# Two cross-attention layers on one core: 120-row chunks in the first layer, transposes issued earlier and singly, a normalisation shared among three engines

## Chip, core, metric

One Trainium2 chip, one core of it. The metric is the device time of the whole kernel in microseconds (us): the median of three runs, and beside it one profiled execution, whose trace gives every other number here. Data are fp32 throughout.

## What is computed

Eight batches. `x` is (8, 100, 1024), the context (8, 1444, 512). Layer 0 is softmax attention over the context with an output projection and a residual; layer 1 is attention whose softmax runs over the 100 queries (axis 1), with a residual and a layer norm.

```python
# layer 0
Q = query @ Wq + bq; K = key @ Wk + bk; V = key @ Wv + bv
weights = softmax(Q @ K.T * 1024**-0.5, axis=-1)
x = query + (weights @ V) @ Wo + bo
# layer 1
q = emb @ Wq + bq; k = latent @ Wk + bk; v = latent @ Wv + bv
w = softmax(q @ k.T / sqrt(1024), axis=1)     # over the queries
x = w @ v + emb
out = (x - mean) * rsqrt(var + 1e-6) * gamma + beta
```

## The kernel before

The kernel multiplies weights together first (Wq with Wk, Wv with Wo), so that scores come straight from `x` and the context, and it forms weights times context (`A`, 512 wide) before it multiplies by the value weights. The large products of weights and the projections use seven half-size products instead of eight (`weight_products`, `queries`, `seven_products`, all through `half_product`, L125). `xT` holds x transposed (1024 features in 8 blocks of 128 partitions, 800 query columns) and takes both residuals.

**Order of work.** TensorE's instructions run in the order in which the program states them (`manual_schedule(engines={PE})`, L65). The other engines' instructions are put in order by the framework's planner, which works with its own costs and may take a later instruction first when an earlier one is not ready; each engine then runs its list strictly in that order. SyncE (SP) issues the context's loads. Loads go into `stream`, ten units that rotate. `bank` gives one of six PSUM banks in turn, `bank2` one of two others.

**First layer.** `scores0` (L493) makes one batch's scores, 44 matmuls, each two issues of TensorE: queries g0T stationary (100 columns), 131 or 132 context columns moving. It yields after each matmul, so that its steps can be put between others. At its last step it emits the softmax: ScalarE evicts (L519), VectorE takes maxima (L520), ScalarE does the exponential (L524) and scales (L527) in `prob`, 100 queries by 1444 positions. The weights must then be transposed, with positions on partitions. `transposed` (L533) has VectorE do this in 32x32 blocks (L542, 16 instructions of up to 12 blocks). For batches 0 and 7, `first_transposed` (L552) has TensorE transpose the first four chunks (L557, `PT = 4`), and ScalarE copies them (L558).

`weighted_rows` (L470) then forms A over 12 chunks of positions: 48 matmuls (L476), context stationary (128 columns), 100 columns of weights moving, one step each. In the first layer a chunk has 128 positions, and the last one 36 (`held_full`), loaded by `load_full_rows` (L430). In the second layer chunks have 120 positions, the last one 124 (`held`), loaded by `load_rows` (L443), which reads 128 rows a chunk at a step of 120 rows.

The main loop of layer 0 first makes the scores of batches 0 and 1 and calls `first_transposed(batches[0])`. Then for each batch b it puts one step of A of b and one step of scores of b+2 alternately (two of the latter at b = 5); the batches 6 and 7 have A alone. `first_transposed(batches[7])` is called at the end of batch 6. `project0` follows.

**Second layer.** `scores1` (L604) has positions on partitions from the start. `attend1` (L670) and, for batches 6 and 7, `weighted_rows` form A. `attended` (L691) transposes it; in batches 6 and 7 ScalarE copies A into A1T directly (L487). `project1_halves` adds the projection of batches 0 to 4 into xT at the end of batch 5; `project1` (L717) that of 5 and 6 at the end of batch 6, eight blocks e of four matmuls (L723), each added by VectorE (L727); it calls `between` after the fourth. `project_last` (L767) does batch 7 (`ol`, L774).

`finish` (L761) makes a batch's output. `untransposed` (L731): eight transposes of TensorE (L738) in two banks, from xT back to 100 rows, and after each four VectorE adds the bias (L740). `statistics`: L745. `normalise` (L747): mean and variance (L750), plus EPS (L752) on VectorE; GpSimd takes the power -1/2 (L753); VectorE forms (z - mean) * gamma (L754), then z * rstd + beta (L758); GpSimd issues the DMA of the output (L759). In batch 7 that last part goes in two halves, issued by SP and ScalarE. `finished` says at which step of which batch `finish` is called whole: batches 0, 1, 2, 3 at steps 0, 12, 26, 40 of batch 6; 4 in the middle of `project1`; 5 and 6 at steps 0 and 16 of batch 7.

## Time and profile before

| | us |
|---|---|
| median of three runs | 662.25 (662.13 to 662.52) |
| the profiled execution | 659.84 |
| its span, first to last instruction | 658.1 |
| first layer's loop, from the first score to project0 | 193.0 to 357.3 |
| last stage, from batch 6 of layer 1 on | 600.8 to 658.1 |
| granted TensorE clock, mean | 0.996 |

Rows of the profile name an engine (PE is TensorE's matmul, PEld its weight load, DVE VectorE, ACT ScalarE, POOL GpSimd, SP SyncE, and a q after it the engine's own queue), the line of the kernel, the operation, the tiles as output<-inputs, the shape, and how many (x). A group's row then has busy time and mean ns of one, and after a second bar the idle time of the engine before it and who ended it. A timeline's row starts with its start and its length in us and merges instructions of the same kind that follow each other. The ends of matmuls are modelled, so the distance between starts says more of TensorE's pace than the lengths.

### The profile page before, as it was taken

To read this page: it belongs to the slowest core of one execution; us is meant where nothing else is said; L and a number is where in the kernel's file an instruction comes from. 1 tells how busy PE (TensorE), PEld (TensorE's weight loads), DVE (VectorE), ACT (ScalarE), POOL (GpSimd) and SP (SyncE) were. 2 spreads that over 40 slices of the span, in tenths; PEclk is the share of its full clock that TensorE was granted. 3 is DMA by queue.
4 is the path that set the end of the run, shared out by engine and by line. 5 is a ranking of instruction groups with operands and counts; after the bars stand their busy time and mean duration, and the time that the engine had idled before them with its cause. 6 is when DMAs were issued, how large, how long until landed. Compare 5 with 4: busy or idle time off the path is not lost.

```text
span 658.1 us, 10293 instructions
## 1 busy us (share of the span) xinstructions
PE 645.4 (98%) x4272; PEld 545.2 (83%) x4272; DVE 404.5 (61%) x771; ACT 120.1 (18%) x313; POOL 27.3 (4%) x37
## 2 busy tenths in 40 slices
PE   9999999999999999999999999999999999999994
PEld 8885445568899999999998555589999999989992
DVE  5979638996054765566742874268344433567994
ACT  1110100321104223321310000214222323210000
POOL 5000000000000000000000000000000000001331
PEclk9999999999999999999999999999999999999998
DMA  9937046000098788888998003038899999810221
GB/s 300 378 123 263 0 129 248 1 0 1 12 355 293 255 290 301 302 300 293 346 330 275 0 0 128 0 105 269 282 313 298 313 293 298 305 58 1 86 66 50
DMA packets 59402, 126.06 MB, mean 192 GB/s; under 512 B 3800, under 2 KB 22744, under 8 KB 59356
## 3 DMA queue, kind: packets, MB, share of 16 engines
q1 hardware_dynamic: 56910, 118.38, 52.4%
q0 software_dynamic: 2048, 6.56, 3.2%
q8 instruction: 33, 0.54, 0.3%
q10 hardware_dynamic: 398, 0.47, 0.2%
q14 instruction: 13, 0.11, 0.0%
HBM read 122.12 MB, written 3.28 MB: 191 GB/s over the span
## 4 chain that ended last, share of the span: by engine, by line
PE 93%; DVE 4%; DMA 1%; issue 1%; POOL 0%; SPq 0%; ACT 0%; POOLq 0%; DVEq 0%
PE A L476 14%; PE s L506 12%; PE s L622 12%; PE A L678 10%; PE qk_x L125 6%; PE g_x L125 5%; PE qk_y L125 4%; PE o_x L125 4%; PE g_y L125 3%; PE vo_x L125 3%; PE o_y L125 3%; PE qk_w L125 2%; PE qk_z L125 2%; PE vo_y L125 2%; PE g_z L125 2%; PE g_w L125 2%
## 5 line engine op out<-in xcount | busy, mean ns | idle before, releaser
L476 PE MATMUL A<-w,c 128*128 128x100 f32 (+1 forms) x960 | 143.9, 269 | 1.2 <-ACT w L558 1.2
L476 PEld LDWEIGHTS A<-w,c 128*128 128x128 f32 (+1 forms) x960 | 127.9, 190 | 3.3 <-ACT w L558 1.6
L622 PE MATMUL s<-g1T,cT 128*120 128x100 f32 (+1 forms) x768 | 123.2, 261 | 0.0
L506 PE MATMUL s<-cT,g0T 128*100 128x131 f32 (+1 forms) x704 | 119.3, 276 | 0.0
L678 PE MATMUL A<-c,w 120*100 120x128 f32 (+1 forms) x576 | 110.7, 273 | 0.0
L622 PEld LDWEIGHTS s<-g1T,cT 128*120 128x120 f32 (+1 forms) x768 | 105.1, 185 | 0.6 <-issue 0.3
L506 PEld LDWEIGHTS s<-cT,g0T 128*100 128x100 f32 x704 | 86.8, 167 | 0.0
L542 DVE STREAM_TRANSPOSE w<-prob 32x352 f32<-32x352 f32 (+3 forms) x128 | 66.5, 519 | 15.3 <-ACT prob L527 12.5
L678 PEld LDWEIGHTS A<-c,w 120*100 120x100 f32 (+1 forms) x576 | 74.0, 168 | 0.0
L642 ACT ACTIVATE w<-w,negmax 120x100 f32<-120x100 f32 (+1 forms) x96 | 35.1, 366 | 75.3 <-DVE negmax L640 75.3
L632 DVE SCALAR_TENSOR_TENSOR w<-s,c 120x400 f32<-120x400 f32 (+1 forms) x24 | 13.8, 573 | 41.6 <-PE s L622 41.6
L519 ACT ACTIVATE prob<-s,c 100x394 f32<-100x394 f32 (+2 forms) x32 | 17.8, 562 | 98.7 <-PE s L506 98.4
L520 DVE TENSOR_REDUCE maxima<-prob 100x1 f32<-100x394 f32 (+2 forms) x32 | 16.4, 528 | 24.3 <-ACT prob L519 24.0
L125 PE MATMUL qk_x<-qk 128*128 128x256 f32 x128 | 28.7, 381 | 0.2 <-DMA qk<-in_L_xattn_WkT 0.2
L125 PEld LDWEIGHTS qk_x<-qk 128*128 128x128 f32 x128 | 23.9, 190 | 4.5 <-issue 0.6
L645 DVE RECIPROCAL rtotal<-total 120x4 f32<-120x4 f32 (+1 forms) x24 | 4.2, 176 | 28.2 <-ACT w L642 28.2
L753 POOL TENSOR_TENSOR rstd<-rstd,mhalf 100x1 f32<-100x1 f32 x8 | 11.8, 1477 | 230.6 <-DVE rstd L752 230.6
L564 DVE TENSOR_TENSOR xT<-xT,o_x 128x400 f32<-128x400 f32 (+1 forms) x24 | 13.7, 603 | 8.3 <-PE o_x L125 7.9
L267 DVE SCALAR_TENSOR_TENSOR qk_L_xattn_bk<-qk,L_xattn_bk,qk_L_xattn_bk 128x1024 f32<-128x1024 f32 x14 | 17.9, 1281 | 0.0
L642 ACT ACTIVATION_READ_ACCUMULATOR w<-w,negmax 120x1 f32 (+1 forms) x96 | 17.9, 186 | 0.0
L659 DVE TENSOR_REDUCE part<-w 120x100 f32<-120x1100 f32 x8 | 17.2, 2147 | 0.0
L332 DVE SCALAR_TENSOR_TENSOR kb<-xT,wqbk,kb 128x400 f32<-128x400 f32 x28 | 16.9, 629 | 0.2
(202 smaller groups left out, 852.8 us busy)
## 6 DMA issues: line engine op xcount, KB each, us to landing
c<-in_ctx SPq DMA_DIRECT2D x48, 768.0 KB, 6.1
cT<-in_ctxT SPq DMA_DIRECT2D x32, 728.0 KB, 6.2
cT<-in_ctxT SPq DMA_DIRECT2D x32, 722.0 KB, 6.4
c<-in_ctx SPq DMA_DIRECT2D x16, 512.0 KB, 8.0
vo<-in_L_xattn_Wo SPq DMA_DIRECT2D x8, 512.0 KB, 5.7
qk<-in_L_xattn_WqT SPq DMA_DIRECT2D x8, 512.0 KB
qk<-in_L_xattn_WqT SPq DMA_DIRECT2D x15, 256.0 KB, 5.4
qk<-in_L_xattn_WkT SPq DMA_DIRECT2D x15, 256.0 KB, 5.8
```

Source lines behind the costliest of these rows:

```text
L125: nc.tensor.matmul(banks[n // per][:, n % per * width : (n % per + 1) * width], lhs[i][:, n * P : (n + 1) * P], rhs[i], start=(fresh and i ...
L267: nc.vector.scalar_tensor_tensor(acc, src, cols[v][:, h : h + 1], acc, ALU.mult, ALU.add)
L332: nc.vector.scalar_tensor_tensor(acc, src, wqbk[:, k : k + 1], acc, ALU.mult, ALU.add)
L476: nc.tensor.matmul(ps[:, k * T : (k + 1) * T], c[m // CQ][:r, m % CQ, k * P : (k + 1) * P], w[:r, m, :], start=(m == 0 and k == 0), stop=( ...
L506: nc.tensor.matmul(banks[n // PM][:T, CUTS[n] - o : CUTS[n + 1] - o], q0[:, k, t0 : t0 + T], cT[k][:, CUTS[n] : CUTS[n + 1]], start=(k == ...
L519: nc.scalar.activation(p[:, o:e], ps[:T, : e - o], AF.Identity, bias=c0[:, b : b + 1], scale=SCALE)
L520: nc.vector.tensor_reduce(parts[:, n : n + 1], p[:, o:e], AX.X, ALU.max)
L542: nc.vector.transpose(blocks(w, r, m0 * T + q * QD, T, n), blocks(p, q, m0 * P + r * QD, P, n),)
L622: nc.tensor.matmul(ps[:r, (m - m0) * T : (m - m0 + 1) * T], cT[m // CQ][:, k, o : o + r], q1[:, k, t0 : t0 + T], start=(k == 0), stop=(k = ...
L642: nc.scalar.activation(w[:r, m, :], w[:r, m, :], AF.Exp, bias=negmax[:r, m : m + 1], accum_out=total[:r, m : m + 1])
L659: nc.vector.tensor_reduce(part[:MR], w[:MR, :last, :].rearrange("p c t -> p t c"), AX.X, ALU.add)
L678: nc.tensor.matmul(ps[:T, part], w[:r, m, :], c[m // CQ][:r, m % CQ, part], start=(m == 0 and k == 0), stop=(m == MC - 1), skip_group_chec ...
```

## The change

It has three parts. The first layer uses `load_rows` and chunks of 120 rows too, `held` everywhere; `load_full_rows` and `held_full` go, and `prob` is 1448 instead of 1472 columns wide. `first_transposed` of batch 0 is called after 40 of the 44 score matmuls of batch 1, and that of batch 7 after 44 of the 48 steps of batch 6, so that four steps follow it. `untransposed` becomes a generator that yields after each transpose; the loop of layer 1 keeps a list of finishing batches and advances each by one transpose after each step of A. Batches 0, 1, 2 start at steps 0, 14, 28 of batch 6, batch 3 is finished whole ahead of `project1`, 4 in its middle as before, 5 and 6 start at steps 6 and 22 of batch 7. z of batches 3 to 5 lies in other buffers (tag gT). In `normalise`, for all batches but the last, ScalarE multiplies z by rstd and GpSimd adds beta, where VectorE did both in L758.

```diff
-SC = -(-S // P)
-SW = (SC - 1) * P + 2 * QD
+SW = (MC - 1) * MR + P
...
-    def load_full_rows(b):
...
-    def held_full(c):
...
-    def weighted_rows(w, c, dst, name, held):
+    def weighted_rows(w, c, dst, name):
...
             for r in range(P // QD):
-                n = SC - m0 - (r * QD >= S % P)
                 nc.vector.transpose(
-                    blocks(w, r, m0 * T + q * QD, T, n),
-                    blocks(p, q, m0 * P + r * QD, P, n),
+                    blocks(w, r, m0 * T + q * QD, T, MC - m0),
+                    blocks(p, q, m0 * MR + r * QD, MR, MC - m0),
                 )
...
         for m in range(PT):
-            nc.tensor.transpose(ps[:, m * T : (m + 1) * T], p[:, m * P : (m + 1) * P], ident[:T, :T])
-        nc.scalar.copy(s["rows"][:, : PT * T], ps[:, : PT * T])
+            nc.tensor.transpose(ps[:MR, m * T : (m + 1) * T], p[:, m * MR : (m + 1) * MR], ident[:T, :T])
+        nc.scalar.copy(s["rows"][:MR, : PT * T], ps[:MR, : PT * T])
...
     def untransposed(s):
         b = s["b"]
-        z = s["z"] = row(f"z_{b}")[:T]
+        if b in range(3, 6):
+            z = work.tile([P, LC, GT], F32, tag="gT", name=f"z_{b}", bufs=3).rearrange("p c t -> p (c t)")[:T, :E]
+        else:
+            z = row(f"z_{b}")[:T]
+        s["z"] = z
         for j in range(2):
             ps = bank(f"z_{b}_{j}")
             for e in range(4):
                 nc.tensor.transpose(ps[:T, e * P : (e + 1) * P], xT[:, 4 * j + e, b * T : (b + 1) * T], ident)
+                if (j, e) != (1, 3):
+                    yield
             half = slice(j * 512, (j + 1) * 512)
             nc.vector.scalar_tensor_tensor(z[:, half], bv1[:T, half], s["r"], ps[:T, :], ALU.mult, ALU.add)
+        yield
...
         nc.vector.scalar_tensor_tensor(z, z, mv[:, 0:1], gamma[:T], ALU.subtract, ALU.mult)
-        parts = 2 if b == B - 1 else 1
-        for j in range(parts):
-            w = slice(j * E // parts, (j + 1) * E // parts)
+        if b < B - 1:
+            nc.scalar.activation(z, z, AF.Copy, scale=rstd)
+            nc.gpsimd.tensor_tensor(z, z, beta[:T], ALU.add)
+            nc.gpsimd.dma_start(out=out[b], in_=z)
+            return
+        for j in range(2):
+            w = slice(j * E // 2, (j + 1) * E // 2)
             nc.vector.scalar_tensor_tensor(z[:, w], z[:, w], rstd, beta[:T, w], ALU.mult, ALU.add)
-            (nc.scalar if j else nc.gpsimd if parts == 1 else nc.sync).dma_start(out=out[b][:, w], in_=z[:, w])
+            (nc.scalar if j else nc.sync).dma_start(out=out[b][:, w], in_=z[:, w])

     def finish(s):
-        untransposed(s)
+        yield from untransposed(s)
...
-    for b in range(2):
-        run(scores0(batches[b], *loaded(load_features(b))))
-    first_transposed(batches[0])
+    run(scores0(batches[0], *loaded(load_features(0))))
+    s0 = scores0(batches[1], *loaded(load_features(1)))
+    for n in range(LC * NP):
+        next(s0)
+        if n == LC * NP - PT - 1:
+            first_transposed(batches[0])
     for b in range(B):
...
-        c, *cT = loaded(load_full_rows(b), *([load_features(b + 2)] if nxt else []))
+        c, *cT = loaded(load_rows(b), *([load_features(b + 2)] if nxt else []))
...
-        if b == B - 2:
-            first_transposed(batches[B - 1])
+            if (b, n) == (B - 2, MC * LC - PT - 1):
+                first_transposed(batches[B - 1])
...
-    finished = {(B - 2, n): (d,) for d, n in enumerate((0, 12, 26, 40))}
-    finished.update({(B - 1, 0): (G1,), (B - 1, 16): (G1 + 1,)})
+    finished = {(B - 2, 0): 0, (B - 2, 14): 1, (B - 2, 28): 2, (B - 1, 6): G1, (B - 1, 22): G1 + 1}
+    finishing = []
...
-            for d in finished.get((b, n), ()):
-                finish(batches[d])
+            if (b, n) in finished:
+                finishing.append(finish(batches[finished[b, n]]))
+            finishing = [f for f in finishing if next(f, finishing) is not finishing]
...
         if b == B - 2:
-            project1(G1, 2, A1[G1][0], lambda: finish(batches[G1 - 1]))
+            run(finish(batches[G1 - 2]))
+            project1(G1, 2, A1[G1][0], lambda: run(finish(batches[G1 - 1])))
```

## Prediction

> **What bounds the kernel now.** I read the page first, then the waits of TensorE, then the timeline of TensorE around each edit, then ScalarE, VectorE and GpSimd in the last 60 us.

> ```profile
> PE 645.4 (98%) x4272; PEld 545.2 (83%) x4272; DVE 404.5 (61%) x771; ACT 120.1 (18%) x313; POOL 27.3 (4%) x37
> ```

> TensorE bounds it: 645.4 of 658.1 us. Some 8 us lie at the start, and 9 us at the end, where the last batch is normalised. Between them its waits that the change can reach are three kinds, 2.9 us in all, shown by the next fence (groups of instructions, columns: busy, mean ns, idle before and who ended it; then two answers of the waits):

> ```profile
> L476 PE MATMUL A<-w,c 128*128 128x100 f32 x704 | 112.8, 266 | 1.2 <-ACT w L558 1.2
> ...
> L476 PE MATMUL A<-w,c 36*128 36x100 f32 x64 | 9.1, 282 | 0.0
> ...
> L738 PE MATMUL z<-ident,xT 128*100 128x128 f32 x64 | 8.5, 273 | 1.2 <-DVE xT L727 1.2
> ...
> PE z L738 <- DVE xT L727: 1.2, 1, 1.2
> PE o L723 <- ACT A1T L487: 0.5, 1, 0.5
> ```

> But a busy TensorE need not be at its pace, so I compare starts. Timeline of TensorE, first layer, the end of batch 0 (start, length, row):

> ```profile
> 232.11 0.39 PE L506 MATMUL s<-cT,g0T 128*100 128x131 f32 x2
> 232.33 0.36 PE L476 MATMUL A<-w,c 128*128 128x100 f32 x2
> 232.53 0.39 PE L506 MATMUL s<-cT,g0T 128*100 128x132 f32 x2
> 232.85 1.53 PE L476 MATMUL A<-w,c 36*128 36x100 f32 x10
> 234.22 0.39 PE L506 MATMUL s<-cT,g0T 128*100 128x131 f32 x2
> ...
> 605.71 3.27 PE L476 MATMUL A<-w,c 120*128 120x100 f32 x28
> 608.81 1.04 PE L738 MATMUL z<-ident,xT 128*100 128x128 f32 x8
> 609.69 3.27 PE L476 MATMUL A<-w,c 120*128 120x100 f32 x28
> ```

> The x10 row holds the eight issues of the 36-row chunk and the next batch's first two. It takes 234.22 - 232.85 = 1.37 us; in the second layer, with 120 rows, 28 such issues take 3.10, 0.111 each, so ten take 1.11. Excess 0.26. Its entry is late too: 0.32 after the s row, where the one before has 0.22. So a 36-row chunk costs **0.36 us a batch** and shows as busy time. Transposes take (609.69 - 608.81)/8 = 0.110 each.

> [...] 36 rows among 128 rows cost 0.36 us for going in and out, while 120 among 128 (second layer) cost nothing visible. [...] here 190 ns with 128 rows, 192 with 120, so 120 rows are no slower. [...]

> **The change, part by part.**

> *Chunks of 120 rows.* There are 12 chunks of either kind, so the same 48 matmuls a batch. Gone is the switch: 8 batches by 0.36 = **-2.9 us**, all on TensorE. Added: loads of 11x128+124 = 1532 rows for 1444, 0.18 MB a batch (+6%), three DMAs on SP for the last quarter instead of two (SP spends 0.4 us on one and is idle for microseconds between them). VectorE's block transposes are all 12 blocks long (568 ns) where half had 11 (538): 64 by 0.03 = 2 us of VectorE spread over 150 us, with 11.8 of 20 us busy in a stage. Both are hidden: a row quarter is issued some 20 us before its use (10 units, 2 used per quarter of a batch) and lands in 6 to 8 us; the second layer moves as many bytes per batch now, at 283 to 307 GB/s and a DMA share of 0.85 to 0.93, and TensorE has no wait there. If the cover were gone: 6.1 MB at 300 GB/s is 20.3 us against a new batch of 19.55, 0.8 us for each of six batches.

> *TensorE's own transposes ahead.* Rows:

> ```profile
> 212.85 0.51 PE L557 MATMUL pT<-ident,prob 100*128 100x100 f32 x4
> 214.00 0.47 PE L476 MATMUL A<-w,c 128*128 128x100 f32 x2 [0.64 <-ACT w L558]
> ...
> 345.06 0.56 PE L557 MATMUL pT<-ident,prob 100*128 100x100 f32 x4
> 346.21 11.13 PE L476 MATMUL A<-w,c 128*128 128x100 f32 x96 [0.58 <-ACT w L558]
> ```

> Four transposes take 0.35, so A could start 0.80 earlier in the first place and 0.74 in the second (0.06 there belongs to the switch above); a first pair after a wait takes 0.30 where later ones take 0.20, 0.10 more each. Sum **-1.7 us**. Now 8 issues follow the transposes: 8 by 0.113 = 0.91 us (scores) or 8 by 0.112 = 0.90 (A), against 0.80 and 0.74 needed. The spare is only 0.1. In the first place ScalarE also evicts batch 1's scores then, at 211.31 to 213.56 without a pause (L519); with the transposes put in after step 40, its third eviction becomes ready later than the copy, so the copy fits between. If it were queued last, 0.9 comes back. The inputs were ready: batch 0's softmax ended at 207.8.

> *Batches one transpose at a time.* Three gains on TensorE:
> (a) finish(3) now stands between the last sums and project1: eight transposes, 0.87 us, fill the wait for the copy of A1T. Row starts 615.21 and 615.95 are 0.74 apart, where 0.11 is due: **-0.6**.
> (b) finish(5) goes from step 0 to step 6 of batch 7. Its eighth transpose now starts at 630.12, seven having started from 627.96 on: 627.96 + 7 x 0.11 = 628.73 was due, **-1.4**. It waits for VectorE's last L727 at 629.71, late because VectorE is full (14.93 of 15 us in 601 to 616, 12.63 of 13 in 616 to 629). The eighth transpose moves 13 steps, 3.5 us, back, and L758 leaves VectorE.
> (c) Mixing. After a group of eight transposes the first two A issues start at 634.70 and 634.79, 0.09 apart, where in a run of A it is 0.112: I read it as room left by the transposes' shorter weight loads. A transpose that stands alone gives that 0.022 each time, a group of eight once. 5 batches by 7 by 0.022 = **-0.8** (between 0 and -0.8; I take -0.8, as the first layer's s and A pairs show it: 0.20 for an A pair among s, 0.224 alone).

> What moves off VectorE: seven L758 of 1.28 us, 9 us, no gain by itself. ScalarE gets seven scalings of 100x1024: L527 takes 1499 ns for 1444, L407 956 for 800, so 1.15 us (estimate, from the slope). GpSimd gets seven adds: [...]

> Gross: 2.9 + 1.7 + 0.6 + 1.4 + 0.8 = **7.4 us**.

> *What is late next.* ScalarE is in order. For each batch the scaling waits for GpSimd's rstd, and behind it stands the copy A1T (L487), for which TensorE waits. In batch 7: from the last transpose of batch 6 to A1T's readiness are 18 steps of 0.224 plus 0.36 = 4.4 us. The scaling's readiness: before, from L740 (636.33) to the end of the pow (640.32) 4.0 us, 0.3 ahead of it; 0.6 less if the first half's statistics no longer come last[...]: 3.7 to 5.1. A tie, so whichever is queued first. If the scaling is (likelier: it comes first in the program), A1T is 0.5 to 1.9 late, less 0.2 that it has to spare (copy ended 642.34, ol started at 642.58). I take **+0.7**. At the end of batch 6 there are 12 steps, 3.0 us, so the copy is ready clearly first; I take 0 and keep 1.6 for the rival.

> Net 7.4 - 0.7 = 6.7. The profiled execution, 659.84 around a span of 658.1, would be 653.1. The median of the runs, 662.25, stands 2.4 above that; the same 6.7 off gives **655.5**.

> **Rivals.**
> 1. *ScalarE's copies become the wait* (chance 0.22). A1T stands behind a scaling in batch 6 (1.6 us) and in batch 7 (1.1), and VectorE[...] leaves no more of (b) than 1.0. For: the tie above, VectorE's full stretch. Against: VectorE gives 9 us away, and ScalarE's queue has already put a ready copy (L558, 213.45) ahead of an exponential that the program has earlier. 655.5 + 1.6 + 0.4 + 0.4 = 657.9.
> 2. *The change does not do what it says in the first layer* (0.07): the copies of part two stay behind other work, or transfers come late. Without part two's 1.7 and with one batch's 0.8: 658.0. All six batches together would be 4.8 us late, less than the 12 us that a quarter has to spare between landing and use.
> 3. *GpSimd becomes the end* (slower; 0.05). Its queue runs from the first pow, about 600, to the last batch's pow, due at 651.08 - 7.4 = 643.7. In 43.6 us stand seven pows and seven DMA issues, 14.4 us, so an add may take 4.2 us. Beyond that each adds seven times its excess to the tail: at 5.2 us the gain is gone, at 6 us the time is 655 + 7 x 1.8 = 667.5. For: no such add was ever timed in the trace. [...]

> **Numbers.** Forecast 655.5, own range 654.2 to 656.9: 0.60. More gain than that (tie goes the other way, a little more from VectorE): 0.06. The rest are the rivals. The range 653.9 to 658.6 leaves out 0.05 below, rival 3, and a little of rival 1. About 0.2%, 1.3 us, is what a measurement of this kernel can tell from no change: faster 0.92, same 0.03, slower 0.05.

> **What would show it.** Right: no L476 row of 36 rows, batches of the first layer 0.36 us apart less; no idle before L476 by L558; no gap at L723 by L487 and none at L738 by L727; transposes in single rows of x1 between pairs of A[...]. Wrong: a wait of ol (L774) or o (L723) on L487 over 1 us, with a scaling just before it on ScalarE; GpSimd busy without a pause up to the tail; a DMA as releaser in the first layer.

## The result and the profile after

| | before | changed |
|---|---|---|
| median, us | 662.19 (661.92 to 662.52, 4 runs) | 653.48 (652.97 to 654.13, 4 runs) |
| profiled execution | 659.84 | 653.41 |
| its span | 658.1 | 651.6 |

The ratio is 0.9869, interval 0.9852 to 0.9886: 8.7 us less. 655.5 was forecast, with 653.9 as the lower end. The two profiled executions differ by only 6.4 us, and that is the riddle of this case: the changed kernel's profiled execution agrees with its median, the one of before stood 2.4 us under its own.

First the stages of the two profiled executions. Each ends where the first matmul of the next starts; the sums are the spans. "Middle" runs from project0 to batch 6 of the second layer, "end" from the first matmul of `project_last`.

| us | to first score | first layer | middle | batch 6 | project1 | batch 7 | end |
|---|---|---|---|---|---|---|---|
| before | 193.00 | 164.27 | 243.49 | 15.19 | 11.81 | 14.82 | 15.49 |
| changed | 193.87 | 160.21 | 243.40 | 14.13 | 11.70 | 13.08 | 15.24 |
| difference | +0.87 | -4.06 | -0.09 | -1.06 | -0.11 | -1.74 | -0.25 |

Without the first column, which the change doesn't touch, 7.3 us are gone; the prediction's sum was 7.4 before its deduction of 0.7.

Page of the changed kernel, engines and the first group (A is L458 now, L476 before):

```profile
PE 641.9 (99%) x4272; PEld 544.1 (84%) x4272; DVE 401.1 (62%) x764; ACT 128.2 (20%) x320; POOL 39.3 (6%) x44
...
L458 PE MATMUL A<-w,c 120*128 120x100 f32 x960 | 145.0, 267 | 0.0
```

No idle time is left before A. Timeline of TensorE, the first transposes of its own (L538) and the end of batch 0:

```profile
212.82 0.51 PE L538 MATMUL pT<-ident,prob 100*120 100x100 f32 x4
213.17 1.07 PE L488 MATMUL s<-cT,g0T 128*100 128x132 f32 x8
214.07 0.36 PE L458 MATMUL A<-w,c 120*128 120x100 f32 x2
...
232.57 0.39 PE L488 MATMUL s<-cT,g0T 128*100 128x132 f32 x2
232.80 1.25 PE L458 MATMUL A<-w,c 124*128 124x100 f32 x10
233.89 0.39 PE L488 MATMUL s<-cT,g0T 128*100 128x131 f32 x2
```

A starts 0.90 us after the first of the eight score issues that now follow the transposes, which is just their own time, 8 by 0.113; no bracket of a wait stands behind its row. The x10 row takes 233.89 - 232.80 = 1.09 us (1.37 before), and it starts 0.23 after the s row (0.32 before): 0.37 us a batch.

The last stage on TensorE (transposes of the outputs are L727, project1 is L704):

```profile
606.94 0.28 PE L727 MATMUL z<-ident,xT 128*100 128x128 f32 x1
607.05 0.36 PE L458 MATMUL A<-w,c 120*128 120x100 f32 x2
607.25 0.27 PE L727 MATMUL z<-ident,xT 128*100 128x128 f32 x1
...
610.64 0.27 PE L647 MATMUL wsum_ps<-ident,wsum 124*100 124x124 f32 x1
610.74 1.04 PE L727 MATMUL z<-ident,xT 128*100 128x128 f32 x8
611.62 5.58 PE L704 MATMUL o<-A1T,wv 128*128 128x200 f32 x32
```

A single transpose and its pair of A take 0.311 us; alone the pair takes 0.223 (issues 0.112 apart in the run of 36 at 631.43), so a transpose costs 0.088 instead of 0.110. project1 starts without a wait, right after the eight transposes of batch 3.

And ScalarE, where I had feared for the copy A1T (L469) behind the scaling (L748):

```profile
631.11 1.15 ACT L748 ACTIVATE z<-z,rstd 100x1024 f32<-100x1024 f32 x1 [5.58 <-POOL rstd L745]
635.68 0.49 ACT L469 COPY A1T<-A 128x400 f32<-128x400 f32 x1 [3.42 <-PE A L458]
636.23 1.15 ACT L748 ACTIVATE z<-z,rstd 100x1024 f32<-100x1024 f32 x1
```

The copy of batch 7 went first, the scaling of batch 6 after it. The loss of 0.7 did not come.

### The profile page after: what moved, and what is told of

Same layout as the page of the kernel before. It is cut to its first block, busy times and chain, and to the rows that moved or that the text cites. A ratio compares the mean times of both kernels' runs of the same rounds, so it can differ in the third digit from the quotient of the medians.

```text
span 651.6 us, 10319 instructions
## 1 busy us (share of the span) xinstructions
PE 641.9 (99%) x4272; PEld 544.1 (84%) x4272; DVE 401.1 (62%) x764; ACT 128.2 (20%) x320; POOL 39.3 (6%) x44
## 4 chain that ended last, share of the span: by engine, by line
PE 58%; issue 35%; POOL 4%; DMA 1%; SPq 0%; POOLq 0%; ACT 0%; DVE 0%; DVEq 0%
PE A L458 12%; PE s L488 12%; PE qk_x L124 6%; PE qk_y L124 4%; PE vo_x L124 3%; PE o_x L124 3%; POOL z L749 3%; PE g_x L124 3%; PE qk_w L124 2%; PE qk_z L124 2%; PE vo_y L124 2%; PE g_y L124 2%; PE o_y L124 1%; PE vo_w L124 1%; PE vo_z L124 1%
## 5 line engine op out<-in xcount | busy, mean ns | idle before, releaser
L458 PE MATMUL A<-w,c 120*128 120x100 f32 x960 | 145.0, 267 | 0.0
L458 PEld LDWEIGHTS A<-w,c 120*128 120x128 f32 x960 | 130.1, 191 | 0.0
L523 DVE STREAM_TRANSPOSE w<-prob 32x384 f32<-32x384 f32 (+1 forms) x128 | 68.6, 536 | 15.3 <-ACT prob L509 12.5
L745 POOL TENSOR_TENSOR rstd<-rstd,mhalf 100x1 f32<-100x1 f32 x8 | 7.5, 934 | 216.5 <-DVE rstd L744 216.4
```

The costliest lines, as they stand in the source:

```text
L458: nc.tensor.matmul(ps[:, k * T : (k + 1) * T], c[m // CQ][:r, m % CQ, k * P : (k + 1) * P], w[:r, m, :], start=(m == 0 and k == 0), stop=( ...
L523: nc.vector.transpose(blocks(w, r, m0 * T + q * QD, T, MC - m0), blocks(p, q, m0 * MR + r * QD, MR, MC - m0),)
```

## The experiments

There are two questions. Do the parts add up as TensorE's stages say, and where do the 2.4 us in the runs of before come from? Theory 1 has it that the stages add up and that the runs of before had something that the profiled execution had not. The rival is a gain that sits outside the stages. Each experiment ran beside the kernel before on the same chip, and the ratios are to these runs.

### The parts alone

`before_again` is the kernel before.

> The kernel before, unchanged. Theory 1 (the profiled execution of before was itself a quick one): its executions spread, and a time near 662.2 us goes with a span near 660.4; the extra is found in a stage that the change doesn't touch, or in the first transfers. Theory 2 (the execution of before was typical, and its runs carry some 2.4 us outside the span): the span is 658 again, with 662 around it.

`rows120`: only the first layer's `load_rows`, `held`, blocks at a step of `MR`.

> Only the first layer's 120-row chunks. Theory 1 (TensorE's stages add up): -2.4 us, which is what the first layer's stage lost in the changed kernel (4.05) without the 1.7 of the transposes ahead; the prediction's own term was -2.9. Theory 2 (part of the gain that the profiles don't show sits in the first layer's loads): -4 to -5 us.

`ahead`: only the two calls of `first_transposed` moved.

> Only TensorE's own transposes earlier, with 128-row chunks. Both theories: -1.7 us, the two idle times before L476 by L558 gone. If the copy fell behind ScalarE's evictions in the first place: -0.8.

`finish`: only `untransposed`, `normalise`, `finish` and their steps.

> Only the finishing: single transposes, new steps, ScalarE and GpSimd in the normalisation. Theory 1: -2.9 (1.06 in batch 6, 0.11 in project1, 1.74 in batch 7), perhaps 0.2 more at the end. Theory 2 (part of the unseen gain sits in the end): -5 us.

| us | median | beside before's 660.63, ratio | first layer | batch 6 | project1 | batch 7 | end |
|---|---|---|---|---|---|---|---|
| before_again | 662.03 | 1.0006 (0.9994 to 1.0018) | 164.26 | 15.19 | 11.81 | 14.81 | 15.48 |
| rows120 | 658.22 | 0.9952 (0.9939 to 0.9965) | 161.94 | 15.20 | 11.81 | 14.82 | 15.47 |
| ahead | 658.96 | 0.9969 (0.9957 to 0.9981) | 162.57 | 15.20 | 11.81 | 14.82 | 15.48 |
| finish | 657.51 | 0.9944 (0.9931 to 0.9957) | 165.89 | 14.13 | 11.71 | 13.08 | 15.20 |

The medians fall by 2.4, 1.7 and 3.1 us, 7.2 in all, and the stages by 2.33, 1.70 and 3.2: theory 1 for the parts. (The intervals of the ratios are about 0.8 us to either side, so the stages are the sharper evidence.) Two things were not expected. The executions of before spread over 2.6 us, from 659.96 to 662.53. And the one profiled of `finish`, which doesn't touch the first layer, has 1.6 us more in it, which the row of the table shows and which is left out of the 3.2. In before_again's own profiled execution (662.12) the extra 2 us are in the first transfers: TensorE stood 1.9 us before its second weights.

### What the row count costs

In the kernel before, the last chunk gets 72 or 64 rows instead of 36 (the diff is shortened):

```diff
# last72, last64: KL = 72 or 64
-        return min(P, S - c * P)
+        return P if c < SC - 1 else KL
...
+                nc.sync.dma_start(out=t[S % P : KL, n, :], in_=src[: KL - S % P, :])
```

> The kernel before with a last chunk of 72 rows instead of 36: rows 36 to 71 carry other rows of the context with weights of zero, so that the result is the same. Theory 1 [...]: -2.9 us, all in the first layer's stage, 164.3 to 161.4, a little under the 161.9 of 120-row chunks. Rival (the unequal chunk, or its separate DMA, costs the time): no change.

> The same with 64 rows. Theory 1: [...] no gain: stage 164.3. If the cost came from any number of rows under some other bound, between 161.4 and 164.3.

Timeline of TensorE at the end of batch 0, last64, then last72:

```profile
233.82 0.39 PE L508 MATMUL s<-cT,g0T 128*100 128x132 f32 x2
234.14 1.53 PE L478 MATMUL A<-w,c 64*128 64x100 f32 x10
235.50 0.39 PE L508 MATMUL s<-cT,g0T 128*100 128x131 f32 x2
```

```profile
233.76 0.39 PE L508 MATMUL s<-cT,g0T 128*100 128x132 f32 x2
233.99 1.26 PE L478 MATMUL A<-w,c 72*128 72x100 f32 x10
235.08 0.39 PE L508 MATMUL s<-cT,g0T 128*100 128x131 f32 x2
```

64 rows: 0.32 to enter and 1.36 for ten, as 36 had. 72 rows: 0.23 and 1.09, as 124 have. The first layer took 164.25 with 64 and 161.51 with 72; the ratios to before are 0.9996 (0.9988 to 1.0005) and 0.995 (0.9935 to 0.9964). So the whole cost hangs on the number of rows: it is there at 36 and at 64 and gone at 72, 2.76 us for eight chunks. The rival falls: the unequal chunk and its extra DMAs are still there in last72. Why 36 and 64 rows have it and 72 have not is not shown. The traces show only the delay, and put 0.35 us on going in and out: in the trace of before the issues of the chunk of 36 rows start 0.11 apart, the first and second at either change of rows 0.20 to 0.21 and 0.19 after the one ahead.

120-row chunks took 161.94, 0.43 more than last72. `both72` is the changed kernel with that last chunk, `after_third` the changed kernel beside it.

> The changed kernel's other two parts with the first layer in 128-row chunks whose last one has 72 rows (36 of them with weights of zero), in place of 120-row chunks. Theory 1 ([...] 120-row chunks give back 0.4 us of pace): the first layer's stage 159.8 in place of 160.2, the rest as in the changed kernel, so 0.4 us less than it. Rival (no difference that can be seen): 160.2 and the same time.

> The changed kernel once more, on the chip of both72, to compare with it. Theory 1: 653.0 to 653.6, in one group, with a clock of 1.00 through the first layer, whatever the runs of before do; its first layer's stage 160.2.

First layer 159.79 against 160.21, every other stage within 0.06. The medians are 652.78 (652.57 to 652.85) and 653.41 (653.02 to 654.15): the four runs of each don't overlap. both72 is the best of all kernels here, 0.9877 (0.9861 to 0.9894) of before on its chip. One round of two score issues and two of A takes 0.4258 us with 120-row chunks and 0.4240 with 128-row ones, on average over some 185 rounds of either trace; the stage has some 240 of them, which makes the 0.43. Why is open.

### Who removed the wait of batch 5

`no_share` is the changed kernel with L748 and L749 put back on VectorE:

```diff
-            nc.scalar.activation(z, z, AF.Copy, scale=rstd)
-            nc.gpsimd.tensor_tensor(z, z, beta[:T], ALU.add)
+            nc.vector.scalar_tensor_tensor(z, z, rstd, beta[:T], ALU.mult, ALU.add)
```

> The changed kernel with rstd and beta on VectorE in one instruction as before. Theory 1 (moving the step off VectorE gains nothing by itself once finish(5) is later): TensorE's stages as in the changed kernel, batch 6 14.13, project1 11.70, batch 7 13.08; its tail the same within 0.3. Rival (VectorE's relief is what removes the wait of the eighth transpose): batch 7 0.5 to 1.5 us longer.

`share_only` is the kernel before with the reverse edit, finishes whole and at the old steps.

> The kernel before with ScalarE and GpSimd in the normalisation, whole finishes at the old steps. Theory 1: batch 6 and project1 as before (15.2 and 11.8); in batch 7 some of the 1.4 us of waiting on L727 goes, since VectorE ends its adds earlier: 13.4 to 14.2 in place of 14.8. Rival ([...] the adds are no earlier): 14.8 or more.

`steps_0_16` is the changed kernel with batches 5 and 6 from steps 0 and 16.

> The changed kernel with batches 5 and 6 finished from steps 0 and 16 of batch 7, as before, but singly. Theory 1: the eighth transpose of batch 5 is at 625.5, after VectorE's last add at 624.5, so no wait; the scaling of batch 6 now comes ahead of the copy A1T on ScalarE and delays it by 0 to 0.5: batch 7 13.1 to 13.5. Rival (the later steps are what removed the wait): 14 or more.

| us | ratio to before on its chip | batch 6 | project1 | batch 7 | end |
|---|---|---|---|---|---|
| changed (after_third) | 0.9888 (0.9873 to 0.9902) | 14.13 | 11.71 | 13.08 | 15.17 |
| no_share | 0.9903 (0.9887 to 0.992) | 14.13 | 12.02 | 13.89 | 15.50 |
| steps_0_16 | 0.9879 (0.9858 to 0.9901) | 14.13 | 11.71 | 13.16 | 15.27 |
| before | 1 | 15.19 | 11.81 | 14.82 | 15.49 |
| share_only | 0.9981 (0.9973 to 0.999) | 15.20 | 11.81 | 13.38 | 15.21 |

All waits of TensorE from the first score on, no_share and then share_only:

```profile
PE z L727 <- DVE xT L708: 0.6, 1, 0.6
```

```profile
PE A L476 <- ACT w L558: 1.2, 2, 0.6
PE o L723 <- ACT A1T L487: 0.5, 1, 0.5
```

In batch 7 of no_share half of the wait is back, six steps later notwithstanding (0.6 where the kernel before has 1.2), and its project1 is 0.31 longer too: weight loads there wait 0.3 for L708. share_only has no wait for VectorE's L727 at all. Its batch 7 is 1.44 shorter than before, the whole of the 1.4, and steps_0_16 loses 0.08 without the later steps. So the rival holds: VectorE's relief is enough to take the wait away, the later steps (with the transposes one at a time) take half of it by themselves, and with the relief they are spare. The 0.08 of steps_0_16 is the tie that I had feared, the other way round: there the scaling of batch 6 runs first, the copy behind it, and the first weights of `ol` wait 0.2 for the copy.

```profile
635.00 1.15 ACT L748 ACTIVATE z<-z,rstd 100x1024 f32<-100x1024 f32 x1 [3.98 <-POOL rstd L745]
636.06 0.47 ACT L469 COPY A1T<-A 128x400 f32<-128x400 f32 x1
```

### The 2.4 us: a window at half clock

In the profiled execution of `finish` the granted clock of TensorE (the share of full speed that it was given) was 0.5 for 3.4 us in the first layer, right behind the second wait for L558. The kernel before has these waits, the changed one has not. These runs were made to see whether the waits do it:

`gap_longer`, the kernel before with a loop of four around the copy.

> The kernel before with the copy L558 done four times, 1.2 us more at both places where TensorE waits for it. Theory 1 (such a wait can make the clock that is granted to TensorE fall to half for 3.4 us, as one execution showed right after this wait): +2.4 us from the waits, and where the clock falls 1.7 us more each time; the windows show a clock under 1 after 214 or 346. Rival (that fall of the clock had nothing to do with the wait): +2.4 and a clock of 1.00 there.

`filled`, the kernel before with work in place of the idle time:

```diff
+        fill = bank(f"fill_{b}")
+        for _ in range(3):
+            nc.tensor.matmul(fill[:, :P], ones, ones, start=True, stop=True)
         nc.scalar.copy(s["rows"][:, : PT * T], ps[:, : PT * T])
```

> The kernel before, with three matmuls of ones (never read) put on TensorE after each of the two groups of its own transposes, so that it works through most of the wait for L558; nothing becomes earlier. Theory 1 (in about half of the executions of before the wait costs a window of 3.4 us at half clock): times near 660.2 throughout, none of the group near 662, clock 1.00 in the stage. Rival (the two groups of times of before come from elsewhere, for example from the first transfers): two groups as before.

`no_ahead`, the changed kernel with the calls back in place:

> The changed kernel with the calls of first_transposed put back to where they were. Theory 1: both waits are back, 1.7 us, and with them the window at half clock in some executions: times near 654.8 and near 656.6. Rival: +1.7 throughout, one group.

Two more executions of before with a trace, and the changed kernel again:

> The kernel before, another execution with its trace. Theory 1: if its time is near 660, the clock is 1.00 in the whole first layer; if it is near 662, the clock is at half for 3.4 us after 214 or 346, or the first transfers were 2 us late (as in the execution of before_again).

> The kernel before, one more execution with its trace. Theory 1: a time near 660 goes with a clock of 1.00 through the first layer, a time near 662 with half clock for 3.4 us after 214 or 346, or with first transfers that are 2 us late.

> The changed kernel, unchanged. Theory 1 (the terms add up, and the runs of before shown with the result were drawn high): 653.4 again, against a median of before near 660.8: -7.3 us, ratio 0.989. Rival (the gain is 8.7): ratio 0.987 again.

The two executions took 661.85 and 661.95 us. TensorE around the second wait in before_look1, ahead of it the last chunk of batch 6:

```profile
344.78 0.72 PE L476 MATMUL A<-w,c 36*128 36x100 f32 x5
345.43 0.56 PE L557 MATMUL pT<-ident,prob 100*128 100x100 f32 x4
346.57 5.67 PE L476 MATMUL A<-w,c 128*128 128x100 f32 x34 [0.58 <-ACT w L558]
```

Stretches of 3.4 us around that wait (columns: stretch and length, busy us and instructions of PE, PEld, DVE, ACT, POOL, then the granted clock, DMA share, GB/s), before_look1, then the first execution of before (659.84), then filled:

```profile
344.10:347.50 3.40, 2.82 (x24) 2.43 (x23) 0.57 (x1) 0.49 (x1) 0.53 (x1) 1.00 0.88 253
347.50:350.90 3.40, 3.40 (x18) 3.40 (x18) 0.00 (x0) 0.00 (x0) 0.00 (x0) 0.50 0.84 312
350.90:354.30 3.40, 3.40 (x32) 3.40 (x32) 0.00 (x0) 0.00 (x0) 0.00 (x0) 1.00 0.65 194
```

```profile
344.10:347.50 3.40, 2.82 (x23) 2.53 (x24) 0.57 (x1) 0.49 (x1) 0.53 (x1) 1.00 0.87 275
347.50:350.90 3.40, 3.40 (x33) 3.40 (x33) 0.00 (x0) 0.00 (x0) 0.00 (x0) 1.00 0.88 308
```

```profile
344.10:347.50 3.40, 3.40 (x30) 3.13 (x29) 0.57 (x1) 0.49 (x1) 0.50 (x1) 1.00 0.92 247
347.50:350.90 3.40, 3.40 (x32) 3.40 (x32) 0.00 (x0) 0.00 (x0) 0.03 (x1) 1.00 0.92 327
```

What else it takes can be read from the traces that have the wait. The times are us from the start of the window in which A goes on after the second wait; a negative one lies in the window ahead.

| trace | rows of the last chunk | its first matmul | A goes on | clock in the next window |
|---|---|---|---|---|
| before_look1 | 36 | 0.31 | 2.52 | 0.5 |
| before_look2 | 36 | 0.44 | 2.64 | 0.5 |
| finish | 36 | 0.90 | 3.11 | 0.5 |
| share_only | 36 | 0.02 | 2.23 | 0.5 |
| before | 36 | -1.88 | 0.33 | 1.00 |
| before_again | 36 | -0.32 | 1.88 | 1.00 |
| last64 | 64 | -0.98 | 1.23 | 1.00 |
| last72 | 72 | 0.59 | 2.57 | 1.00 |
| no_ahead | 124 | 0.17 | 2.15 | 1.00 |
| rows120 | 124 | -1.51 | 0.47 | 1.00 |

The clock fell where one window held the whole chunk of 36 rows and the whole wait, and nowhere else. last72 and no_ahead have the same wait inside one window behind a chunk of more rows, and it didn't fall. Nor did it after the first wait, 0.64 us long and behind score matmuls of 128 rows, in any trace of these ten. From the first matmul of the chunk to A are 2.21 us, so the window's start has 3.41 - 2.21 = 1.2 us in which both fit. If every place of the start is as likely as any other, 35% of the executions fall: an estimate from these traces.

How often do they fall? The record has the mean clock of every run beside the experiments. Of 86 runs of before, 29 had 0.993 or 0.994, with a median of 662.02 us; the other 57 had more and a median of 660.43. That is 34%. `share_only`, which has both the chunk and the wait, falls into two groups as well: 8 of its 20 runs have spans of 658.2 to 658.8 and a mean clock of 0.994 or 0.995, the others 656.4 to 657.8 and more. The two conditions can be taken away one at a time:

- *The chunk without the wait.* `filled` has its median at 660.53, and none of its 14 runs is at 0.993 or 0.994, while 7 of 19 runs of before on its chip are. Nothing in it is earlier, its first layer is 164.26; only TensorE is kept at work. `ahead` had none in 9. (In the traced execution of filled the chunk lies across two windows, so its fence shows only that the idle time is gone; it is the 14 runs that count.)
- *The wait without the chunk of 36 rows.* rows120, last72 and no_ahead had none in 13 runs, last64 none in 12.

(A mean of 0.995 doesn't decide: the traced executions of finish and share_only have it with the window, that of filled without.) So both the idle time and the chunk of few rows just ahead of it are shown to be needed, and each of the change's first two parts removes the window. Why the rows count is not shown, and whether 64 rows are few enough rests on 12 runs alone, since the one trace of last64 has its chunk across two windows.

after_again (653.03) and after_third stay in one group, eight runs from 652.88 to 654.15. The ratio of after_again, 0.9872 (0.9848 to 0.9895), is what its rival expected, but because 5 of the 7 runs of before on its chip had the window; after_third, with 1 of 7, has 0.9888. no_ahead had 654.98 (654.88 to 655.17) and a first layer of 161.94, 1.73 more, as expected, and in four runs none in a second group: theory 1 had overlooked that the changed kernel has no chunk of 36 rows.

gap_longer missed: 673.25, +11 for +2.4 expected. The planner put the repeated copies in between the softmax's steps, where ready copies stood behind steps that were waiting for VectorE,

```profile
221.12 0.75 PE L476 MATMUL A<-w,c 128*128 128x100 f32 x2 [7.42 <-ACT w L559]
...
357.47 7.79 PE L476 MATMUL A<-w,c 128*128 128x100 f32 x44 [2.15 <-ACT w L559]
```

so the waits were 8.3 us longer in all. The remaining 5.2 of the 13.6 us by which the first layer is longer (177.83 us) are the clock, at half for some 5.4 us of work after either wait (column of the clock: 0.53 and 0.51):

```profile
216.00:227.00 11.00, 5.88 (x31) 5.89 (x32) 7.49 (x16) 3.75 (x5) 0.00 (x0) 0.53 0.10 37
...
356.00:363.00 7.00, 5.53 (x26) 5.53 (x27) 0.00 (x0) 1.36 (x3) 0.40 (x1) 0.51 0.54 182
```

It agrees with theory 1 at the second place, where the wait was 2.2 us; the 7.4 us of the first tell little of a wait of 0.6.

Late first transfers (2 us in before_again) are a second source of spread, one that the changed kernel has too. Four of the 86 runs of before were over 661.2 us without the low clock; what held them up is not on record.

## Why the prediction was wrong, step by step

The step that failed is the last: "The median of the runs, 662.25, stands 2.4 above that; the same 6.7 off gives 655.5". I took the distance between profiled execution and median as a constant of the kernel. The greater part of it was a term of the change: 1.6 of the 2.4 us are the window at half clock, which executions of before near 662 have and the profiled one had not, and some 0.6 is what the runs without it (660.43) stand above that quick execution. The change removes the wait and the chunk of 36 rows, and with them the window. The four runs shown with the result lie at 661.92 to 662.52; their clock is not on record, so that each had the window is inferred, but all 17 of the 86 others between 661.9 and 662.6 had it. That all four fell there, where a third of the others did, is chance or a matter of their chip. Against executions of before without the window the changed kernel is 7.0 us faster, against those with it 8.5. For the idle time ahead of L476 I put down its own length; the second wait could be worth 1.6 more.

Without that step the sum gives 653.1 for the profiled execution, and 653.41 was measured. That is closer than the sum deserves: the first column took 0.9 more by luck (in the traces of all these kernels it lies anywhere from 193.0 to 195.0), and the 0.7 of loss did not come.

The terms of the sum:
- *120 rows*: -2.9 predicted, -2.33 measured in rows120. The cost of the 36 rows was right, 2.76 (last72) for the 2.9; the 0.43 that the 120 rows give back was not in it. "120 rows are no slower" was drawn from the weight loads alone (in the trace of before 190 ns with 128 rows, 192 with 120). The 6% more bytes were hidden, as said: no wait for a DMA in the first layer of the changed kernel.
- *Transposes ahead*: -1.7, measured -1.70. The copy L539 ran at 213.37 between the second and third eviction, as reckoned. That the wait was also one of the two conditions of the half clock was not in it.
- *(a)* and *(c)*: batch 6 lost 1.06, 0.6 and three times 0.16 being predicted; a single transpose gains the 0.022 that *(c)* took. (In the trace of before the weight load of a transpose takes 130 ns on average, that of a 120-row A 192. That the gain comes from there was my reading and is not shown.)
- *(b)*: -1.4, size right, cause half wrong. It named both the later steps and L758 leaving VectorE, but then gave the relief of VectorE "no gain by itself"; the relief alone brings it all (share_only -1.44), and no_share, with the later steps alone, still waits 0.6. That the two together gave no more than 1.4 made the size come out all the same.
- *What is late next*: +0.7 predicted, 0 measured. The upper end of the 3.7 to 5.1 us, like the 1.0 for *(b)* in rival 1, was my estimate; the trace of before shows neither. GpSimd's queue decided the tie: the power of batch 6 began only after the add and the DMA of batch 5 and ended at 636.20, so the copy, at 635.68, went first. Where the order is the other way (steps_0_16) it costs 0.08, so the price was too high as well.
- *GpSimd*: the trace of before had no add to go by. In that of the changed kernel an add takes 2.35, well under the 4.2 that rival 3 allows, and the end was never in danger. (Rival 3's 655 + 7 x 1.8 is 667.6, not 667.5.)

The net of 6.7 against 7.3 is the smaller part of the miss of 2.0; the clock is the larger. The range reached 1.6 below the forecast. That left room for the 0.7 of loss that didn't come, but not for 1.6 of half clock on top of it, a gain that the profile of one execution without the window couldn't show.

## What to carry to other kernels

A short wait of TensorE can cost more than its length. Here 0.58 us behind matmuls of 36 rows cost 1.6 us more, in a third of the executions and not in the others. So when a profiled execution is quicker than the median, ask what the median has before carrying the distance on; the mean clock of each run is a place to look. Read TensorE's pace from starts and from counts in a stretch: the delay at a chunk of few rows (0.35 us here) and half a clock (1.6) both show as busy. And where an engine is full, taking work off it and moving its consumer later both work on the same wait: only a run with one of them alone shows what each is worth.

## What the runs showed of the hardware beside that

In the changed kernel VectorE's L746 (inputs z and gamma) takes longer where GpSimd's add L749 runs beside it, 2.68 us instead of 1.27. First L746, then GpSimd's add and its power L745:

```profile
616.13 2.68 DVE L746 SCALAR_TENSOR_TENSOR z<-z,mv,prob 100x1024 f32<-100x1024 f32 x1
...
629.38 1.27 DVE L746 SCALAR_TENSOR_TENSOR z<-z,mv,prob 100x1024 f32<-100x1024 f32 x1
```

```profile
615.37 2.35 POOL L749 TENSOR_TENSOR z<-z,prob 100x1024 f32<-100x1024 f32 x1 [1.26 <-ACT z L748]
...
618.65 0.58 POOL L745 TENSOR_TENSOR rstd<-rstd,mhalf 100x1 f32<-100x1 f32 x1
...
629.55 1.52 POOL L745 TENSOR_TENSOR rstd<-rstd,mhalf 100x1 f32<-100x1 f32 x1 [0.69 <-DVE rstd L744]
```

With no add beside it, L746 takes the 1.27 us. Beside the add that ends at 617.72 it takes 2.68 and ends 1.1 after the add. The changed kernel has five such cases. L746 takes 1.46 to 2.68 us in them, and in all five it ends 1.08 us after the add, so it did most of its 1.27 us of work only then. The other way, the power takes 0.58 when it comes late and 1.52 when it starts with L746; either way it ends 0.42 us after L746 (which ends at 618.81 and 630.65). In the kernel before it ends 0.42 to 0.43 after its partner L754 in all eight batches, so most of its 1.46 there fits a wait for VectorE.
